# A convolution, attention and mixture-of-experts kernel: attention's matrix by halves of the channels, the norm's mean added to the residual by VectorE, the output's base made by ScalarE

## The chip, the cores and the metric

The kernel runs on one core of a Trainium2 chip. The metric is the device time in microseconds from the first to the last instruction. The core has a matrix engine (TensorE, PE in the profile, with its weight loads as PEld), a vector engine (VectorE, DVE), a scalar engine (ScalarE, ACT), a general one (GpSimd, POOL) and a queue that starts transfers (SyncE, SP). Each engine works through its own instructions in order, and they wait for one another through semaphores.

## The reference, cut to what matters

The input is 8 images of 56 x 56 pixels with 256 channels. Layer 0 is a convolution block: 32 parallel paths, each 256 to 4 channels, a 3 x 3 convolution, and back to 256, each step with a batch norm and a relu; the paths are summed and the input is added. Layer 1 reads its output as 3136 tokens for each image. The change lies in the middle of layer 1.

```python
x = relu(sum_of_paths(x) + x)                       # layer 0
t = x.reshape(8, 3136, 256)
n = ln(t)                                           # (t - mean) / sqrt(var + eps), over 256 channels
k = head_norm(n); v = head_norm(n)                  # 8 heads of 32 channels
kv = einsum('bhnd,bhne->bhde', k, v) / 3136         # one 32 x 32 matrix a head and image
t = t + einsum('bhnd,bhde->bhne', n, kv) + n        # attention, linear in n
u = ln(t)
t = t + u + sum_over_2_of_8_experts(gate * (gelu(u @ w1 + b1) @ w2 + b2))
```

Two facts carry the change. The attention's matrix, kv by heads with the identity added (A in the kernel), is block diagonal: a head of 32 channels reads only its own 32 channels, so output channels 0 to 127 need only input channels 0 to 127. And n = (t - mean) * rs1, so that A applied to n is rs1 * (t A) minus rs1 * mean * (the column sums of A): the mean can be taken into the matrix, or added afterwards as one row times one number for each token.

## The kernel before, in words

The work is cut into 56 chunks of 448 tokens (8 rows of pixels), seven for each image. A chunk lies in SBUF with tokens on the partitions, as 4 groups (k) of 112 tokens, or with channels on the partitions, as 2 halves (f) of 128.

The program is a loop over slots s = 0 to 64. In slot s the convolution's last product runs on chunk s (`conv3_steps`), its first product on chunk s + 2, its 3 x 3 product on chunk s + 1, the end of the convolution and the keys on chunk s - 1 (`end_steps`), and the attention on chunk a = s - 8 (`attn_steps`): an image's attention can only begin when all seven chunks of it have given their part of kv. `image_steps` makes A and its tables once an image, in the slot of its first chunk. `route_steps` chooses two experts for each token of the two chunks before, and scatters token rows to regions sorted by expert. `moe_steps` works through tiles of 256 such rows: transposes (te), two products (ph, py) with gelu between, and an indirect transfer by POOL that adds the result to the output rows. Slots 8 to 55 hold both convolution and attention; 56 to 64 hold attention and tiles alone; then only tiles are left.

Within a slot the order of PE, ACT and DVE is written out: `issue` (L1368) gives each part a stretch of the slot, spreads its steps over that stretch in proportion to their costs, and emits them sorted. The attention has 0.05 to 0.97 of a slot, or 0.35 to 0.97 in a slot that opens an image. POOL's and SP's orders are left to the framework. The three ordered engines then run strictly in that order, so a late step holds all that stands behind it on its engine.

The convolution's last product sets the beat. A `pair` (L577) is two products of 448 columns into two PSUM banks (c), a relu on ACT (L592) and a maximum and sum on DVE (L595) into r; `sum_paths` (L601) adds four r by a product (su), and when a half of the channels is done DVE adds bias and input (u, L615). Then `begin` (L643) is a relu of u on ACT, and `turn` (L655) transposes it on PE (tu). Seven PSUM banks serve all products except su.

The attention of one chunk, in `attn_steps`:
- `attend(k)`, four times: PE multiplies 112 tokens by the table tab of 256 + 16 columns (at, L870), once for each half f of the input channels, summed in PSUM. The table holds A with its column means taken off in all 256 columns, so the half away from the diagonal holds only the negative means. The last 16 columns are router logits. DVE multiplies by rs1 and adds the residual X (L874), ACT copies the logits (L878), and DVE takes mean and variance (L881, L882).
- After the fourth, POOL makes rs2 as a power of -0.5 (L885), and `means` makes nm = -mean * rs2 on DVE (L889).
- `normed(k)`: ACT writes the normed tokens to pay (L894), which is what routing scatters.
- `base`: POOL adds X and pay (L900) and SP stores the sum to the output (L902). The tiles later add their results to those rows.

`matrix` (L800) computes A's column means (cs) by a product with a constant matrix, A's transpose for the router, and fills the table with six DVE operations (L816, L818, L819).

Of the kernel before, what the change touches and what calls it, by code (L numbers as in the profile page):

```python
# [25 lines left out]
def kernel(  # L26
# [513 lines left out]

    below = const.tile([P, M, M], F32, name="below")
    nc.gpsimd.memset(below, 1.0)
# [89 lines left out]

    spilled, rs1s, kvs = {}, {}, {}
    G = KT * NH

    def end_steps(s):
# [58 lines left out]
        def variances():  # L695

            sd = v["sd"] = small([T, KT, NH + 1], "hsd")
            ss = small([T, KT, NH], "hss")
            nc.vector.tensor_reduce(
                ss, v["sq"].rearrange("q k (h c) -> q (k h) c", c=HC), AX.X, ALU.add  # L700
            )
            m = v["m"]
            mu = small([T, KT], "hmu")
            dm = small([T, KT, NH], "hdm")
            nc.vector.tensor_reduce(mu, m, AX.X, ALU.add)
            nc.vector.scalar_tensor_tensor(
                dm, mu[:, :, None].to_broadcast([T, KT, NH]), -1.0 / NH, m,
                op0=ALU.mult, op1=ALU.add,
            )
            nc.vector.tensor_mul(dm, dm, dm)  # L710
            nc.vector.scalar_tensor_tensor(
                dm, dm, float(HC), ss, op0=ALU.mult, op1=ALU.add
            )
            nc.vector.tensor_reduce(mu, dm, AX.X, ALU.add)
            nc.vector.tensor_scalar(
                sd[:, :, NH], mu, 1.0 / C, LN_EPS, ALU.mult, ALU.add
            )
            nc.vector.tensor_scalar_mul(sd[:, :, :NH], ss, 1.0 / (HC - 1))  # L718
            nc.gpsimd.tensor_tensor(  # L719
                sd, sd, half[:T, :].rearrange("q (k h) -> q k h", k=KT), ALU.pow  # L720
            )

        def inverse():
# [8 lines left out]
            rs1s[s] = keep.tile([T, KT], F32, tag="rs1", name=f"rs1_{s}")  # L732
            nc.vector.reciprocal(rs1s[s], sd[:, :, NH])

        def scale():
# [26 lines left out]

    tables_of = {}

    def image_steps(b):

        v = {}
# [32 lines left out]
        def matrix():  # L800
# [4 lines left out]
            for f in range(NF):  # L805
                nc.tensor.matmul(ps[:, f, :], mean_of, A[:, f, :], start=True, stop=True)
                nc.tensor.transpose(pt[:, f, :], A[:, f, :], ident)
            tab = v["tab"] = one.tile(
                [P, NF, C + 2 * E], F32, tag="tab", name=f"tab_{b}", bufs=2
            )  # L810
            nc.vector.tensor_copy(AT, pt)
            for f in range(NF):
                for g in range(NF):
                    dst = tab[:, f, g * P : (g + 1) * P]
                    if f == g:
                        nc.vector.tensor_sub(dst, A[:, g, :], ps[:, g, :])  # L816
                    else:
                        nc.vector.tensor_scalar_mul(dst, ps[:, g, :], -1.0)  # L818
                nc.vector.tensor_copy(tab[:, f, C + E :], rwc[:, f, :])  # L819

        def router():
# [13 lines left out]
            for f in range(NF):  # L835
                nc.vector.tensor_sub(tab[:, f, C : C + E], AR[:, f, :], pm[:, :E])
            tables_of[b] = tab

# [14 lines left out]
    def attn_steps(a):  # L853
        b, c = divmod(a, NCH)
        v = {}
        X, tT = Xs[a], fetched.pop(a)
        rs1 = rs1s.pop(a)
        lg = keep.tile([T, KT, 2 * E], F32, tag="lg", name=f"lg_{a}", bufs=4)
# [4 lines left out]
        nm = stat.tile([T, KT], F32, tag="nm", name=f"nm_{a}")  # L863
        late = []

        def attend(k):

            ps = ps_mm.tile([T, C + 2 * E], F32, tag="mm", name=f"at_{a}_{k}")
            for f in range(NF):
                nc.tensor.matmul(  # L870
                    ps, tT[:, f, k * T : (k + 1) * T], tables_of[b][:, f, :],
                    start=(f == 0), stop=(f == NF - 1),
                )
            nc.vector.scalar_tensor_tensor(  # L874
                X[:, k, :], ps[:, :C], rs1[:, k : k + 1], X[:, k, :],
                op0=ALU.mult, op1=ALU.add,
            )
            late.append(lambda: nc.scalar.copy(lg[:, k, :], ps[:, C:]))  # L878
            if k:
# [7 lines left out]
        def means():  # L887
            late.pop(0)()
            nc.vector.scalar_tensor_tensor(  # L889
                nm, mv[:, :, 0], -1.0, rs2, op0=ALU.mult, op1=ALU.mult  # L890
            )

        def normed(k):
# [3 lines left out]
            )  # L897

        def base():
            nc.gpsimd.tensor_add(X, X, pay[:, :, :C])  # L900
            del Xs[a]
# [7 lines left out]

        return (  # L910
            [(1.0, lambda k=k: attend(k)) for k in range(KT)]
            + [(0.6, means)]
            + [(0.4, lambda k=k: normed(k)) for k in range(KT)]
            + [(0.6, base)]
        )

# [10 lines left out]
    def route_steps(group):  # L927
# [10 lines left out]
        def logit():  # L938
            lg = v["lg"] = small([E], "rlg")
            for n, m in enumerate(group):  # L940
                _, raw, rs1, _ = pays[m]
                mine = lg[:, n * KT : (n + 1) * KT, :]
                nc.vector.tensor_tensor(
                    mine, raw[:, :, :E], rs1[:, :, None].to_broadcast([T, KT, E]), ALU.mult
                )
                nc.vector.tensor_add(mine, mine, raw[:, :, E:])

# [560 lines left out]
```

## Time and profile before

The three runs took 3394.81, 3409.42 and 3416.62 us; the median is 3409.42 us. The profiled execution has a span of 3400.0 us and a mean granted TensorE clock of 0.946.

| what | value |
|---|---|
| attention's products (at, L870) | 896 records, 265.7 us busy, mean 420 ns |
| their weight loads | 896 records, 148.8 us busy, mean 181 ns |
| residual on DVE (L874) | 224, 106.9 us, mean 477 ns |
| norm to pay on ACT (L894) | 224, 135.0 us, mean 604 ns |
| base on POOL (L900) | 56, 129.1 us, mean 2305 ns |
| power for rs2 on POOL (L885) | 56, 63.1 us, mean 1127 ns |
| r on DVE (L595) | 1792, 1127.3 us, mean 677 ns |
| r on ACT (L592) | 1792, 1031.9 us, mean 636 ns |

How to read the lines below. A row of the groups names line, engine, operation, output <- inputs, shapes and count; then the total busy time in us and the mean ns of one; then the idle time of that engine just before these instructions, with what ended most of it. A row of the stretches has start and end in us, the length, and for PE, PEld, DVE, ACT and POOL the busy us with the count of instructions, then granted clock, share of the transfer engines, and GB/s. A row of the waits says which instruction waited for which: total us, times, longest. A row of the timeline has start and length in us, engine, line, operation and tiles, how many alike were merged, and in brackets the idle time before and what ended it. Matmuls overlap, and their ends are modelled.

### The profile page before, as it was taken

The numbers are of one execution on the slowest core, as the hardware profiler recorded it, in microseconds if no ns is written. First come the engines' busy times: TensorE is split into PE (matmuls) and PEld (weight loads), VectorE is DVE, ScalarE is ACT, GpSimd is POOL, SyncE is SP. The second block draws the span as 40 slices with busy tenths as digits, with TensorE's granted clock in tenths as the row PEclk, the third lists the DMA queues.
The fourth block names the chain that finished last, engine by engine and source line by source line (L and its number), as shares of the span: only waits on it lengthen the run. The fifth ranks groups of instructions, "written<-read, shape, count | busy, mean of one in ns | idle before, by whom it ended". The sixth has DMA issues, their size and how long they took to land. (4 is left out here: it accounts for less than half of the span.)

```text
span 3400.0 us, 55203 instructions
## 1 busy us (share of the span) xinstructions
PE 3012.4 (89%) x16669; PEld 1697.1 (50%) x16669; DVE 2200.1 (65%) x5806; ACT 1894.1 (56%) x3799; POOL 1926.1 (57%) x1385
## 2 busy tenths in 40 slices
PE   5888888878999999999998999999999988788698
PEld 2333433333444554545455555455454545676587
DVE  4566777777777767776776777776777775333200
ACT  1555555546565665656665666566656655343345
POOL 2123234453456575656656566656656666777677
PEclk7999888889999999999998999999999999898899
DMA  5522244434556675666666676566666756788797
GB/s 119 136 83 79 77 113 122 123 101 143 147 150 158 163 186 160 173 159 175 167 167 173 155 199 182 153 174 180 168 168 158 189 149 176 174 224 220 178 224 177
DMA packets 341577, 537.72 MB, mean 158 GB/s; under 512 B 60048, under 2 KB 251680, under 8 KB 341280
## 3 DMA queue, kind: packets, MB, share of 16 engines
q1 hardware_dynamic: 257952, 430.73, 43.6%
q0 software_dynamic: 81984, 103.45, 16.8%
q8 instruction: 134, 2.20, 0.3%
q14 instruction: 163, 1.34, 0.1%
q10 hardware_dynamic: 1344, 0.02, 0.0%
HBM read 248.01 MB, written 192.55 MB: 130 GB/s over the span
## 5 line engine op out<-in xcount | busy, mean ns | idle before, releaser
L595 DVE SCALAR_TENSOR_TENSOR r<-c,nb,r 128x448 f32<-128x448 f32 x1792 | 1127.3, 677 | 563.0 <-ACT r L592 538.5
L592 ACT ACTIVATE r<-c,b3t 128x448 f32<-128x448 f32 x1792 | 1031.9, 636 | 394.8 <-PE c L587 378.1
L1325 POOL DMA_INDIRECT out_dram<-y,index x420 | 662.5, 1577 | 355.8 <-ACT y L1311 243.7
L587 PE MATMUL c<-hl,W3hl 64*128 64x448 f32 x3584 | 712.1, 431 | 71.8 <-ACT r L592 43.0
L608 PE MATMUL su<-r,gather 128*32 128x448 f32 x3584 | 582.0, 574 | 67.5 <-DVE r L595 67.1
L1031 POOL DMA_INDIRECT regions<-pay,rrowi x448 | 432.7, 966 | 322.2 <-PE c L587 211.4
L587 PEld LDWEIGHTS c<-hl,W3hl 64*128 64x128 f32 x3584 | 344.5, 190 | 507.7 <-issue 202.0
L1287 PE MATMUL ph<-eT,w 128*128 128x256 f32 x1680 | 462.4, 406 | 57.2 <-DMA w<-Wd 23.9
L1307 PE MATMUL py<-w,hT 128*128 128x256 f32 x1680 | 433.5, 383 | 0.0
L1311 ACT ACTIVATE y<-py,g 128x256 f32<-128x256 f32 x420 | 196.5, 474 | 398.0 <-PE py L1307 348.6
L1287 PEld LDWEIGHTS ph<-eT,w 128*128 128x128 f32 x1680 | 304.1, 197 | 196.9 <-issue 88.8
L719 POOL TENSOR_TENSOR hsd<-hsd,half 112x36 f32<-112x36 f32 x56 | 351.8, 6283 | 78.0 <-DVE hsd L718 77.6
L1291 ACT ACTIVATE hT<-ph,w 128x256 f32<-128x256 f32 x420 | 197.8, 476 | 300.2 <-PE ph L1287 180.9
L1307 PEld LDWEIGHTS py<-w,hT 128*128 128x128 f32 x1680 | 292.5, 192 | 28.2
L681 POOL TENSOR_TENSOR norm<-t,hmean 112x512 f32<-112x512 f32 x112 | 120.2, 1132 | 320.4 <-PE c L587 180.7
L870 PE MATMUL at<-tab,tT 128*112 128x272 f32 x896 | 265.7, 420 | 11.6 <-ACT y L1311 7.0
L608 PEld LDWEIGHTS su<-r,gather 128*32 128x32 f32 x3584 | 105.3, 110 | 275.9 <-DVE r L595 158.9
L262 PE MATMUL c<-R,W2t 96*32 96x448 f32 x1344 | 186.9, 573 | 13.2 <-DMA R<-h 11.8
L870 PEld LDWEIGHTS at<-tab,tT 128*112 128x112 f32 x896 | 148.8, 181 | 91.7 <-issue 16.3
L1303 PE MATMUL py<-b2hl,own 128*128 128x256 f32 x420 | 177.8, 423 | 18.5 <-ACT hT L1291 8.0
L894 ACT ACTIVATE pay<-X,nm,rs 112x256 f32<-112x256 f32 x224 | 135.0, 604 | 91.9 <-DVE nm L889 91.9
L976 POOL TENSOR_TENSOR rq<-ebase,rq 112x8 f32<-112x8 f32 (+1 forms) x32 | 52.9, 1654 | 197.7 <-DVE rq L975 197.7
(245 smaller groups left out, 3225.1 us busy)
## 6 DMA issues: line engine op xcount, KB each, us to landing
w<-Wd SPq DMA_DIRECT2D x210, 513.0 KB
rows<-regions SPq DMA_DIRECT2D x210, 259.0 KB
xi<-in_x_dram SPq DMA_DIRECT2D x56, 448.0 KB
hl<-hi SPq DMA_DIRECT2D x448, 56.0 KB
hl<-lo SPq DMA_DIRECT2D x448, 56.0 KB
tTs<-u SPq DMA_DIRECT2D x56, 448.0 KB
ts<-t SPq DMA_DIRECT2D x56, 448.0 KB
tT<-tTs SPq DMA_DIRECT2D x56, 448.0 KB
```

Source lines behind the costliest of these rows:

```text
L587: product = nc.tensor.matmul(tiles[g][:, :CH], W3hl[rows, ab, cg, :], hl[rows, ab, :], start=True, stop=True)
L592: nc.scalar.activation(r, tiles[0][:, :CH], AF.Relu, bias=b3t[:, cg, 2 * ab : 2 * ab + 1])
L595: nc.vector.scalar_tensor_tensor(r, tiles[1][:, :CH], nb3[:, cg, 2 * ab + 1 : 2 * ab + 2], r, op0=ALU.max, op1=ALU.add,)
L608: nc.tensor.matmul(ps[32 * c4 : 32 * c4 + 32, :CH], gather, unit.pop((s, 4 * u + c4)), start=(ab == 0), stop=(ab == NQ - 1),)
L719: nc.gpsimd.tensor_tensor(sd, sd, half[:T, :].rearrange("q (k h) -> q k h", k=KT), ALU.pow)
L870: nc.tensor.matmul(ps, tT[:, f, k * T : (k + 1) * T], tables_of[b][:, f, :], start=(f == 0), stop=(f == NF - 1),)
L1031: ins = nc.gpsimd.indirect_dma_start(out=regions[n], out_offset=bass.IndirectOffsetOnAxis(ap=v["row_i"][:, (m - group[0]) * KT + k, n : n ...
L1287: nc.tensor.matmul(ps, w[:, f * C + hf * P : f * C + (hf + 1) * P], eT[:, f, :], start=(f == 0), stop=(f == NF - 1),)
L1291: nc.scalar.activation(hT[:, hf, :], ps, AF.Gelu, bias=w[:, 2 * NF * C + hf : 2 * NF * C + hf + 1])
L1307: nc.tensor.matmul(ps, hT[:, f, h * P : (h + 1) * P], w[:, (NF + f) * C : (NF + f + 1) * C], start=False, stop=(f == NF - 1),)
L1311: nc.scalar.activation(y[:, h, :], ps, AF.Identity, scale=g[:, h : h + 1])
L1325: ins = nc.gpsimd.indirect_dma_start(out=out_rows, out_offset=at, in_=y[:, h, :], in_offset=None, compute_op=ALU.add, **partial,).ins
```

## The change: what it does and what it is for

Attention's matrix by halves. The table now holds, for each half f, only the 128 columns of its own diagonal block of A and the 16 logit columns, 144 in all. The two products of an attend no longer add up in PSUM: each writes its own 144 columns. The aim is fewer columns streamed by PE. The logits come in two halves, which `logit` adds on DVE.

The mean by VectorE. As A is stored without its means taken off, the means are added to the residual instead: `center` does X = cm * shift + X once for each k, where cm is the row of A's column means, the same on all partitions, and shift is -(sum of the token's channels) * rs1, made in `variances` and `inverse`. `matrix` then only copies.

The base by ScalarE. `raised(k)` computes X * (rs2 + 1) + nm, which is X plus its norm, on ScalarE in place of the addition on GpSimd; `up` is rs2 + 1. The steps' costs, by which `issue` places them, change with it: the four attends now fill a smaller part of the attention's stretch.

One constant of the planning (below) becomes bfloat16, which makes room in SBUF.

```diff
-    below = const.tile([P, M, M], F32, name="below")
+    below = const.tile([P, M, M], BF16, name="below")
...
+            v["sum"] = small([T, KT], "hsum")
+            nc.vector.tensor_scalar_mul(v["sum"], mu, -float(HC))
...
+            shifts[s] = keep.tile([T, KT], F32, tag="shift", name=f"shift_{s}")
+            nc.vector.tensor_mul(shifts[s], v["sum"], rs1s[s])
...
             nc.vector.tensor_copy(AT, pt)
-            for f in range(NF):
-                for g in range(NF):
-                    dst = tab[:, f, g * P : (g + 1) * P]
-                    if f == g:
-                        nc.vector.tensor_sub(dst, A[:, g, :], ps[:, g, :])
-                    else:
-                        nc.vector.tensor_scalar_mul(dst, ps[:, g, :], -1.0)
-                nc.vector.tensor_copy(tab[:, f, C + E :], rwc[:, f, :])
+            nc.vector.tensor_copy(cm, ps)
+            nc.vector.tensor_copy(tab[:, :, :P], A)
+            nc.vector.tensor_copy(tab[:, :, P + E :], rwc)
...
+        def center():
+
+            cm = tables_of[b][1].rearrange("q f c -> q (f c)")
+            for k in range(KT):
+                nc.vector.scalar_tensor_tensor(
+                    X[:, k, :], cm[:T], shift[:, k : k + 1], X[:, k, :],
+                    op0=ALU.mult, op1=ALU.add,
+                )
+
         def attend(k):
 
-            ps = ps_mm.tile([T, C + 2 * E], F32, tag="mm", name=f"at_{a}_{k}")
+            ps = ps_mm.tile([T, NF, NT], F32, tag="mm", name=f"at_{a}_{k}")
             for f in range(NF):
                 nc.tensor.matmul(
-                    ps, tT[:, f, k * T : (k + 1) * T], tables_of[b][:, f, :],
-                    start=(f == 0), stop=(f == NF - 1),
-                )
+                    ps[:, f, :], tT[:, f, k * T : (k + 1) * T], tables_of[b][0][:, f, :],
+                    start=True, stop=True,
+                )
+            mine = X[:, k, :].rearrange("q (f c) -> q f c", f=NF)
             nc.vector.scalar_tensor_tensor(
-                X[:, k, :], ps[:, :C], rs1[:, k : k + 1], X[:, k, :],
-                op0=ALU.mult, op1=ALU.add,
-            )
-            late.append(lambda: nc.scalar.copy(lg[:, k, :], ps[:, C:]))
+                mine, ps[:, :, :P], rs1[:, k : k + 1], mine, op0=ALU.mult, op1=ALU.add
+            )
+            late.append(lambda: nc.scalar.copy(lg[:, k], ps[:, :, P:]))
...
+            nc.vector.tensor_scalar_add(up, rs2, 1.0)
...
+        def raised(k):
+
+            nc.scalar.activation(
+                X[:, k, :], X[:, k, :], AF.Identity,
+                bias=nm[:, k : k + 1], scale=up[:, k : k + 1],
+            )
+
         def base():
-            nc.gpsimd.tensor_add(X, X, pay[:, :, :C])
...
         return (
-            [(1.0, lambda k=k: attend(k)) for k in range(KT)]
+            [(0.1, center)]
+            + [(1.0, lambda k=k: attend(k)) for k in range(KT)]
             + [(0.6, means)]
             + [(0.4, lambda k=k: normed(k)) for k in range(KT)]
-            + [(0.6, base)]
+            + [(0.4, lambda k=k: raised(k)) for k in range(KT)]
+            + [(0.1, base)]
         )
...
+                nc.vector.tensor_add(raw[:, :, 0], raw[:, :, 0], raw[:, :, 1])
```

More of the change, by code (lines that the diff above doesn't have):

```diff
@@ L630, in conv3_steps @@
         return steps
-    spilled, rs1s, kvs = {}, {}, {}
+    spilled, rs1s, shifts, kvs = {}, {}, {}, {}
     G = KT * NH
@@ L763 @@
     tables_of = {}
+    NT = P + 2 * E
     def image_steps(b):
@@ L807, in matrix @@
                 nc.tensor.transpose(pt[:, f, :], A[:, f, :], ident)
-            tab = v["tab"] = one.tile(
-                [P, NF, C + 2 * E], F32, tag="tab", name=f"tab_{b}", bufs=2
-            )
+            tab = v["tab"] = one.tile([P, NF, NT], F32, tag="tab", name=f"tab_{b}", bufs=2)
+            cm = v["cm"] = one.tile([P, NF, P], F32, tag="cm", name=f"cm_{b}", bufs=2)
             nc.vector.tensor_copy(AT, pt)
-            for f in range(NF):
-                for g in range(NF):
-                    dst = tab[:, f, g * P : (g + 1) * P]
-                    if f == g:
-                        nc.vector.tensor_sub(dst, A[:, g, :], ps[:, g, :])
-                    else:
-                        nc.vector.tensor_scalar_mul(dst, ps[:, g, :], -1.0)
-                nc.vector.tensor_copy(tab[:, f, C + E :], rwc[:, f, :])
+            nc.vector.tensor_copy(cm, ps)
+            nc.vector.tensor_copy(tab[:, :, :P], A)
+            nc.vector.tensor_copy(tab[:, :, P + E :], rwc)
         def router():
@@ L835, in router @@
             for f in range(NF):
-                nc.vector.tensor_sub(tab[:, f, C : C + E], AR[:, f, :], pm[:, :E])
-            tables_of[b] = tab
+                nc.vector.tensor_sub(tab[:, f, P : P + E], AR[:, f, :], pm[:, :E])
+            tables_of[b] = (tab, v["cm"])
         return [(1.0, keys), (1.5, matrix), (1.0, router)]
@@ L856, in attn_steps @@
         X, tT = Xs[a], fetched.pop(a)
-        rs1 = rs1s.pop(a)
-        lg = keep.tile([T, KT, 2 * E], F32, tag="lg", name=f"lg_{a}", bufs=4)
+        rs1, shift = rs1s.pop(a), shifts.pop(a)
+        lg = keep.tile([T, KT, NF, 2 * E], F32, tag="lg", name=f"lg_{a}", bufs=4)
         pay = payp.tile([T, KT, ROW], F32, tag="pay", name=f"pay_{a}")
@@ L863, in attn_steps @@
         nm = stat.tile([T, KT], F32, tag="nm", name=f"nm_{a}")
+        up = stat.tile([T, KT], F32, tag="up", name=f"up_{a}")
         late = []
+        def center():
[5 more added lines that the diff above has]
+                )
         def attend(k):
-            ps = ps_mm.tile([T, C + 2 * E], F32, tag="mm", name=f"at_{a}_{k}")
+            ps = ps_mm.tile([T, NF, NT], F32, tag="mm", name=f"at_{a}_{k}")
             for f in range(NF):
                 nc.tensor.matmul(
-                    ps, tT[:, f, k * T : (k + 1) * T], tables_of[b][:, f, :],
-                    start=(f == 0), stop=(f == NF - 1),
+                    ps[:, f, :], tT[:, f, k * T : (k + 1) * T], tables_of[b][0][:, f, :],
+                    start=True, stop=True,
                 )
+            mine = X[:, k, :].rearrange("q (f c) -> q f c", f=NF)
             nc.vector.scalar_tensor_tensor(
-                X[:, k, :], ps[:, :C], rs1[:, k : k + 1], X[:, k, :],
-                op0=ALU.mult, op1=ALU.add,
+                mine, ps[:, :, :P], rs1[:, k : k + 1], mine, op0=ALU.mult, op1=ALU.add
             )
-            late.append(lambda: nc.scalar.copy(lg[:, k, :], ps[:, C:]))
+            late.append(lambda: nc.scalar.copy(lg[:, k], ps[:, :, P:]))
             if k:
@@ L942, in logit @@
                 mine = lg[:, n * KT : (n + 1) * KT, :]
+                nc.vector.tensor_add(raw[:, :, 0], raw[:, :, 0], raw[:, :, 1])
                 nc.vector.tensor_tensor(
-                    mine, raw[:, :, :E], rs1[:, :, None].to_broadcast([T, KT, E]), ALU.mult
+                    mine, raw[:, :, 0, :E], rs1[:, :, None].to_broadcast([T, KT, E]), ALU.mult
                 )
-                nc.vector.tensor_add(mine, mine, raw[:, :, E:])
+                nc.vector.tensor_add(mine, mine, raw[:, :, 0, E:])
         dsc = desc[:T, None, :].to_broadcast([T, K, E])
```

## The prediction

> **What bounds the kernel now.** I read the page's shares first, then the busy time by stretches, then who PE waits for, then single slots of the timeline, and only then the rows of the lines that change.
>
> ```profile
> PE 3012.4 (89%) x16669; PEld 1697.1 (50%) x16669; DVE 2200.1 (65%) x5806; ACT 1894.1 (56%) x3799; POOL 1926.1 (57%) x1385
> ```
>
> The busiest engine is PE, but the mean hides stages. The busy time by stretches, with the columns PE, PEld, DVE, ACT, POOL, granted clock, DMA share and GB/s:
>
> ```profile
> 400.00:2800.00 2400.00, 2208.21 (x12551) 1156.58 (x12550) 1776.23 (x4529) 1435.95 (x2868) 1389.14 (x943) 0.96 0.60 158
> 3000.00:3200.00 200.00, 147.40 (x728) 124.78 (x727) 60.19 (x291) 78.04 (x178) 148.63 (x115) 0.86 0.77 200
> ```
>
> From 400 to 2800 us, the slots in which convolution and attention run together, PE is busy 92% and DVE 74%. From 2800 on, DVE is light, POOL and the DMA are busy three quarters of the time, and PE 74 to 89%. So PE work taken away counts in the first stretch, unless DVE is what a slot waits for. What PE waits for there (total us, times, longest):
>
> ```profile
> PE su L608 <- DVE r L595: 52.8, 32, 3.2
> PE c L587 <- ACT r L592: 27.1, 46, 2.6
> ```
>
> When PE stands, it mostly stands for DVE. One slot in two, about, shows why. In slots that route two chunks, DVE is nearly full for long stretches, here the first 10 us and then 1657 to 1667 us:
>
> ```profile
> 1642.50:1647.50 5.00, 5.00 (x32) 2.98 (x32) 4.68 (x16) 3.86 (x9) 1.24 (x1) 1.00 1.08 322
> 1647.50:1652.50 5.00, 5.00 (x27) 2.72 (x26) 4.76 (x15) 3.42 (x6) 0.00 (x0) 1.00 0.81 254
> 1657.50:1662.50 5.00, 4.78 (x28) 2.51 (x28) 4.82 (x12) 2.73 (x7) 2.35 (x3) 1.00 0.82 183
> 1662.50:1667.50 5.00, 4.48 (x20) 1.76 (x19) 4.86 (x17) 2.81 (x7) 2.46 (x4) 1.00 0.50 139
> ```
>
> The rows of what the change touches:
>
> ```profile
> L870 PE MATMUL at<-tab,tT 128*112 128x272 f32 x896 | 265.7, 420 | 11.6 <-ACT y L1311 7.0 <-ACT r L592 4.2
> L747 PE MATMUL kv<-norm 112*128 112x129 f32 x896 | 131.2, 306 | 21.2 <-DVE r L595 18.0 <-POOL norm L737 1.1 <-ACT r L592 0.3
> L894 ACT ACTIVATE pay<-X,nm,rs 112x256 f32<-112x256 f32 x224 | 135.0, 604 | 91.9 <-DVE nm L889 91.9
> L900 POOL TENSOR_TENSOR X<-X,pay 112x1024 f32<-112x1024 f32 x56 | 129.1, 2305 | 34.6 <-ACT pay L894 34.2
> L874 DVE SCALAR_TENSOR_TENSOR X<-at,rs,X 112x256 f32<-112x256 f32 x224 | 106.9, 477 | 69.6 <-PE at L870 69.3
> ```
>
> The attention's 448 matmuls show as 896 records: each float32 matmul runs as two. The kv row has the same count at 129 columns instead of 272, a near twin of the new width of 144.
>
> [...] the four records of one attend take 1.17 us with 0.39 us for one, so (1.17 - 0.39)/3 = 0.26 us apart[...]; sixteen of kv take 2.05 us, 0.116 us apart[...]. [...] small copies into pay (L1019) take 171 ns in the median and up to 3.0 us.
>
> **The change part by part.**
>
> *Halves on PE.* The two records of one product fall from 272 to 144 columns each. [...] by the slope between the two rows' spacings ((0.26 - 0.116)/143 = 1.0 ns a column) 129 ns and 115 us. I take 96, which is 1.71 us for each of 56 chunks. Of the chunks, 48 run beside the convolution and 8 in the tail.
>
> *Centre on VectorE.* Four new scalar_tensor_tensor of 112x256 per chunk, by the neighbour L874 0.48 us each: 1.9 us[...]. Five small operations come with it (the head sum, the shift, the raised scale, one addition of the two logit halves, each near 0.19 us or less): 0.7 us. Together 2.6 us on DVE for each chunk, 147 us in all. Where this lands decides the case. In the changed order the four stand right behind the slot's first two r and, in routing slots, six small logit operations, and in front of the u of L615. Behind u queue ScalarE's relu of it (L643), PE's turn of u (L655), and everything after on PE, which runs in order. Both kinds of slot, DVE rows first:
>
> ```profile
> 1700.39 0.68 DVE L615 SCALAR_TENSOR_TENSOR u<-su,sumb,xT 128x448 f32<-128x448 f32 x1
> 1702.70 1.28 DVE L595 SCALAR_TENSOR_TENSOR r<-c,nb,r 128x448 f32<-128x448 f32 x2 [1.64 <-ACT r L592]
> ...
> 1747.91 0.68 DVE L615 SCALAR_TENSOR_TENSOR u<-su,sumb,xT 128x448 f32<-128x448 f32 x1
> ```
>
> ```profile
> 1749.19 0.96 ACT L643 ACTIVATE u<-u 128x896 f32<-128x896 f32 x1
> ```
>
> ```profile
> 1750.73 0.65 PE L655 MATMUL tu<-ident,u 128*112 128x128 f32 x4 [0.75 <-ACT r L592]
> ```
>
> In the plain slot (1700 us) DVE stands idle 1.64 us right after u: the four additions cost nothing, hidden by that idle time. In the routing slot (1747 us) u ends at 1748.59 and ScalarE takes it 0.6 us later, PE's turn starts 0.58 us after ScalarE's end and has waited already. Put 1.9 us and two logit additions of 0.19 us ahead: u ends 2.3 us later, ScalarE 1.7 us later, PE's turn about 1.2 us later than now, and PE came there 0.43 us sooner, so it stands 1.6 us longer. That is the saving of 1.71 us, given back. In the slots that open an image the centre comes later, but into a stretch where DVE is also full; its 1.9 us are set against some 0.5 us that the shorter table saves (six operations, in the rows of L816, L818 and L819 two each of 277, 284 and 163 ns, 1.4 us an image, for two wide copies like L811's 0.41 us and one narrow). I count no gain there.
>
> *Base on ScalarE.* Four activations like pay's, 0.60 us each, 2.4 us a chunk, 135 us in all, on an engine busy 60% in the main stretch. They stand one by one between r, y and hT at the slot's end, where DVE has little to do; each can delay an r by 0.6 us, and I count nothing, with up to 0.5 us a slot in the range. POOL loses its addition of 2.3 us, 129 us in all, which in the main stretch nobody but the store waits for.
>
> *Tail.* Eight chunks save 1.71 us of PE, of which half counts with PE not the only limit: 7 us. There VectorE waits 82 us for the power of rs on POOL (L885), because that stands behind scatters and the old addition. Without the addition, and with the power some four scatters earlier in POOL's order in the routing slots, I count 6 us.
>
> *The rest*, the mask in bfloat16 and the wider logits, lies in small operations and costs nothing that shows.
>
> *Sum.* 21 plain slots at 1.71 us: 36. 20 routing and 7 opening slots: 0. Tail 7 + 6 = 13. 3409 - 49 = 3360 us.
>
> **The rivals.** *The whole gain comes* (chance 0.20): 96 us of PE, and 8 x 2.2 us of POOL in the tail, 3409 - 114 = 3295. For it: 92% PE. Against it: the routing slot above. *DVE and ScalarE take it all* (0.25): the plain slots give 36 us, but 0.5 us a slot of ScalarE's new work (24 us) comes back, and 3409 - 12 - 0 = about 3397. For it: PE waits for r from both engines. *Slower* (0.13): in routing and opening slots DVE is the bound and the full 2.6 us lands on the path: 27 x 2.6 = 70 us, less 36 us of the plain slots, 3443. For it: DVE at 4.7 to 4.9 of 5 us; against it: DVE runs idle again for 1.05 to 2.7 us within each such slot. My own case has 0.42.
>
> **How the numbers follow.** 3360 is the likeliest case. The lower end, 3295, is the full gain; the upper, 3430, lies between no change and the slower case, and leaves out most of that. Over 1% faster is below 3375: the full gain and most of my case, 0.54. Within 1% (to 3443): 0.31. Slower by more: 0.15.
>
> **What would show it.** The attention's records: 896 with 0.12 to 0.13 us between them, mean near 0.31 us. The centre's row: 224 of about 0.48 us. In plain slots DVE's idle time after u gone, and the slot about 1.7 us shorter; in routing slots PE waiting longer in front of the turn of u, and the slot as long as before. The wait of VectorE for the power in the tail below 82 us. I am wrong if routing slots shorten as well (then PE absorbed the late u), if plain slots don't, if the centre's additions take much more than 0.48 us beside POOL's work, or if the granted clock (0.96) moves by some per cent.

## The result, and the profile after

The changed kernel takes 3523.06 us in the median of four runs (3521.86 to 3525.01); the kernel before, run beside it, takes 3407.84. The ratio is 1.034, interval 1.031 to 1.038: 115 us slower, where 49 us faster was forecast.

First the shares of the page:

```profile
PE 3064.6 (87%) x16669; PEld 1729.8 (49%) x16669; DVE 2308.7 (66%) x6230; ACT 1996.1 (57%) x4023; POOL 1802.3 (51%) x1329
```

PE is busy 52 us longer than before, although its new products are shorter. The busy time by stretches, for the main stretch:

```profile
400.00:2800.00 2400.00, 2136.01 (x11851) 1122.26 (x11849) 1774.81 (x4632) 1443.14 (x2882) 1196.80 (x837) 0.94 0.56 149
```

In this stretch PE is busy 72 us less than before in the same one and finishes 700 records fewer, at a granted clock of 0.94 where it was 0.96. The groups of what changed:

```profile
L881 PE MATMUL at<-tab,tT 128*112 128x144 f32 x896 | 166.9, 310 | 0.3
...
L872 DVE SCALAR_TENSOR_TENSOR X<-cm,shift,X 112x256 f32<-112x256 f32 x224 | 99.6, 506 | 0.0
...
L913 ACT ACTIVATE X<-X,nm,up 112x256 f32<-112x256 f32 x224 | 133.2, 608 | 0.0
```

Each of these is close to the forecast: the products fell by 265.7 - 166.9 = 98.8 us, the additions take 0.51 us on average, ScalarE's part 133 us. What changed beside them is in the waits of the same stretch:

```profile
PE c L587 <- ACT r L592: 72.1, 59, 9.0
ACT pay L906 <- DVE nm L900: 59.1, 7, 10.0
PE su L608 <- DVE r L595: 53.0, 39, 4.0
...
PE tu L655 <- ACT r L592: 35.0, 15, 2.4
```

The last of these waits was this before:

```profile
PE tu L655 <- ACT r L592: 10.4, 14, 0.8
```

PE stands longer for ScalarE's r (the first row was 27.1 us before), and ScalarE for nm (28.4 us before). To see where, I cut the trace at the first of the 64 products c of each slot and summed the slots by kind: those that open an image, plain ones, those that route two chunks, and routing ones before an opening. The last column is the time within slots 8 to 55 that the trace's clock record gives at half clock; slot 55 ends with its last product c. Each row is one profiled execution; in slots 0 to 7, which have no attention, the kernels differ by -4 to +7 us. Lengths of before in us, then differences to it:

| kernel | 0-7 | 8-14 | opening (6) | plain (18) | routing (12) | routing, next opens (5) | tail | half clock |
|---|---|---|---|---|---|---|---|---|
| before | 327.0 | 323.0 | 392.5 | 842.7 | 645.4 | 257.7 | 553.9 | 191 |
| after | +5.0 | +25.3 | +39.9 | +20.7 | +28.9 | +16.7 | -16.4 | 297 |
| costs only (e1) | +1.9 | +12.0 | +21.4 | +6.6 | +22.3 | +5.8 | +3.2 | 256 |
| old places (e2) | +5.8 | +16.9 | +18.8 | +2.1 | +36.1 | +23.1 | -15.8 | 348 |
| halves only (e5) | -3.8 | -3.4 | +12.9 | +2.8 | +0.6 | +5.8 | +1.0 | 287 |
| base only (e6) | -3.6 | -2.1 | +11.7 | +11.2 | -9.0 | +1.0 | -14.9 | 198 |
| centre only (e7) | -0.8 | +3.6 | +8.7 | +4.8 | +20.4 | +7.8 | +5.3 | 205 |
| centre in the gap (i1) | +6.8 | +2.1 | +16.5 | +23.6 | +2.5 | +9.9 | -17.3 | 236 |
| warm openings (i3) | +3.3 | -7.4 | -9.5 | +1.9 | -2.7 | +0.7 | -8.1 | 109 |

**A routing slot of after** (28), on VectorE, ScalarE and PE, and the stretches over the same time:

```profile
1438.92 1.67 DVE L872 SCALAR_TENSOR_TENSOR X<-cm,shift,X 112x256 f32<-112x256 f32 x4
1440.50 0.68 DVE L615 SCALAR_TENSOR_TENSOR u<-su,sumb,xT 128x448 f32<-128x448 f32 x1
...
1441.21 0.95 ACT L643 ACTIVATE u<-u 128x896 f32<-128x896 f32 x1 [1.41 <-DVE u L615]
1442.07 1.14 ACT L592 ACTIVATE r<-c,b3t 128x448 f32<-128x448 f32 x2
...
1439.38 0.94 PE L587 MATMUL c<-hl,W3hl 64*128 64x448 f32 x4
1442.74 0.65 PE L655 MATMUL tu<-ident,u 128*112 128x128 f32 x4 [2.42 <-ACT r L592]
1443.32 1.96 PE L608 MATMUL su<-r,gather 128*32 128x448 f32 x8
1445.21 2.56 PE L225 MATMUL c<-xT,W1s 128*128 128x448 f32 x4
```

```profile
1441.00:1443.00 2.00, 0.26 (x2) 0.27 (x3) 1.86 (x8) 1.79 (x3) 0.00 (x0) 1.00 1.05 312
1443.00:1445.00 2.00, 2.00 (x12) 0.47 (x10) 1.86 (x7) 0.79 (x2) 0.00 (x0) 0.60 0.80 293
1445.00:1447.00 2.00, 2.00 (x4) 0.99 (x4) 1.90 (x6) 0.00 (x0) 0.00 (x0) 0.54 0.01 4
1447.00:1449.00 2.00, 2.00 (x14) 1.27 (x12) 0.78 (x7) 1.20 (x3) 1.40 (x1) 1.00 0.00 0
```

The four additions stand ahead of u; ScalarE waits 1.41 us for u, its r stands behind, and PE waits 2.42 us where the kernel before waited 0.75. The new thing follows: of the next four microseconds some 3.4 are at half clock (0.60 and 0.54 in the two stretches), su takes 1.96 us and c 2.56. In the routing slot of before that the prediction shows, these two followed the turn of u like this:

```profile
1751.31 0.96 PE L608 MATMUL su<-r,gather 128*32 128x448 f32 x8
1752.20 1.77 PE L225 MATMUL c<-xT,W1s 128*128 128x448 f32 x4
```

So the wait is paid twice, once standing and once in slow products.

**An opening slot of after** (36, from 48.1 us after its start), on POOL, VectorE, ScalarE and PE:

```profile
1926.91 6.17 POOL L722 TENSOR_TENSOR hsd<-hsd,half 112x36 f32<-112x36 f32 x1
...
1935.60 1.64 POOL L896 TENSOR_TENSOR rs<-rs,mhalf 112x4 f32<-112x4 f32 x1
...
1937.27 0.16 DVE L900 SCALAR_TENSOR_TENSOR nm<-mv,rs 112x4 f32<-112x4 f32 x1 [3.35 <-POOL rs L896]
...
1937.47 0.60 ACT L906 ACTIVATE pay<-X,nm,rs 112x256 f32<-112x256 f32 x1 [5.52 <-DVE nm L900]
...
1938.64 1.26 PE L587 MATMUL c<-hl,W3hl 64*128 64x448 f32 x2 [5.61 <-ACT pay L906]
1939.84 2.07 PE L1308 MATMUL ph<-eT,w 128*128 128x256 f32 x4
```

Power of hsd, a scatter and an indirect addition, power of rs, nm, pay, r, product: one chain, and PE stands 5.61 us. Here too the products behind the wait are slow, ph takes 2.07 us at a granted clock of 0.50 (1938 to 1942 us).

### The profile page after: what moved, and what is told of

It reads as the page before. It is cut to its first block, busy times and chain, and to the rows that moved or that the text cites. A ratio compares the mean times of both kernels' runs of the same rounds, so it can differ in the third digit from the quotient of the medians.

```text
span 3520.2 us, 55737 instructions
## 1 busy us (share of the span) xinstructions
PE 3064.6 (87%) x16669; PEld 1729.8 (49%) x16669; DVE 2308.7 (66%) x6230; ACT 1996.1 (57%) x4023; POOL 1802.3 (51%) x1329
## 5 line engine op out<-in xcount | busy, mean ns | idle before, releaser
L587 PE MATMUL c<-hl,W3hl 64*128 64x448 f32 x3584 | 775.2, 435 | 119.5 <-ACT r L592 90.2
L608 PE MATMUL su<-r,gather 128*32 128x448 f32 x3584 | 629.6, 590 | 97.8 <-DVE r L595 72.3
L587 PEld LDWEIGHTS c<-hl,W3hl 64*128 64x128 f32 x3584 | 370.7, 191 | 553.6 <-ACT r L592 240.3
L1308 PE MATMUL ph<-eT,w 128*128 128x256 f32 x1680 | 471.8, 413 | 25.5 <-ACT hT L1312 7.6
L1328 PE MATMUL py<-w,hT 128*128 128x256 f32 x1680 | 440.9, 388 | 0.0
L681 POOL TENSOR_TENSOR norm<-t,hmean 112x512 f32<-112x512 f32 x112 | 121.6, 1164 | 329.8 <-PE c L587 132.5
L608 PEld LDWEIGHTS su<-r,gather 128*32 128x32 f32 x3584 | 115.7, 111 | 327.4 <-DVE r L595 169.3
L262 PE MATMUL c<-R,W2t 96*32 96x448 f32 x1344 | 193.1, 556 | 13.5 <-DMA R<-h 11.2
L881 PEld LDWEIGHTS at<-tab,tT 128*112 128x112 f32 x896 | 124.2, 182 | 95.2 <-issue 45.2
L881 PE MATMUL at<-tab,tT 128*112 128x144 f32 x896 | 166.9, 310 | 0.3
```

The costliest lines, as they stand in the source:

```text
L587: product = nc.tensor.matmul(tiles[g][:, :CH], W3hl[rows, ab, cg, :], hl[rows, ab, :], start=True, stop=True)
L608: nc.tensor.matmul(ps[32 * c4 : 32 * c4 + 32, :CH], gather, unit.pop((s, 4 * u + c4)), start=(ab == 0), stop=(ab == NQ - 1),)
L881: nc.tensor.matmul(ps[:, f, :], tT[:, f, k * T : (k + 1) * T], tables_of[b][0][:, f, :], start=True, stop=True,)
L1308: nc.tensor.matmul(ps, w[:, f * C + hf * P : f * C + (hf + 1) * P], eT[:, f, :], start=(f == 0), stop=(f == NF - 1),)
L1328: nc.tensor.matmul(ps, hT[:, f, h * P : (h + 1) * P], w[:, (NF + f) * C : (NF + f + 1) * C], start=False, stop=(f == NF - 1),)
```

## The experiments

Each ratio is to the kernel before, run beside it, with its 95% interval. That kernel's median lay between 3398.9 and 3407.8 us from one set of runs to the next, so small differences between sets are better read from the ratios.

**Where the steps stand (e1 to e4).** The change also altered the list of step costs, and so where every step of the attention stands. e1 gives the kernel before the new list, with empty steps in place of the new ones:

```
-            [(1.0, lambda k=k: attend(k)) for k in range(KT)]
+            [(0.1, lambda: None)]
+            + [(1.0, lambda k=k: attend(k)) for k in range(KT)]
...
-            + [(0.6, base)]
+            + [(1.6, lambda: None)]
+            + [(0.1, base)]
```

> The kernel before with nothing changed but the attention's list of step costs: the list of the changed kernel, with empty steps where centre and raised stand (0.1 and 1.6). No instruction is added or taken away; attends, means and normed move earlier in the slot. Theory 'placement' (the steps moved to where PE, ACT and POOL cannot follow): 60 to 100 us slower than before, 3470 to 3510, most of it in the slots that open an image (ScalarE holding its first pay until the power of rs2 is there). Rival 'work' (VectorE's and ScalarE's added work is what costs): within 1% of before, 3375 to 3440.

3475.92 us, ratio 1.0224 (1.0207 to 1.0241). The list alone costs 77 us: opening slots 3.6 us each, where pay's first activation again stands ahead of r and waits for the power, routing slots 1.9.

e2 is the changed kernel with a list that puts the steps where they stood:

```
-            [(0.1, center)]
+            [(0.0, center)]
...
-            + [(0.4, lambda k=k: raised(k)) for k in range(KT)]
-            + [(0.1, base)]
+            + [(0.15, lambda k=k: raised(k)) for k in range(KT)]
+            + [(0.0, base)]
```

> The changed kernel with the attends, means and normed back at their places of before (centre costs 0.0, raised 0.15 each, base 0.0, the sum 6.8 as before). All of the new work stays. Theory 'placement': 60 to 100 us faster than the changed kernel, 3420 to 3465; the slots that open an image lose their extra 7 us, the routing slots keep the late u. Rival 'work': no different from the changed kernel, 3500 to 3535.

3487.82 us, 1.0259 (1.0242 to 1.0276). It lies between the two expectations: only 35 us come back, or 26 when each kernel is set against the kernel before beside it. Placement and the rest overlap; a cost of 89 us remains at the old places.

e3 keeps the new list and puts each addition directly ahead of its own residual; e4 does both:

```
+            center(k)
             mine = X[:, k, :].rearrange("q (f c) -> q f c", f=NF)
```

> The changed kernel with its step costs, but each of the four centre operations stands directly before the residual's operation of its own attend, so none stands before u. Theory 'late u' (the four in front of u hold ScalarE's relu of u and PE's turn of it): the routing slots lose the 2.9 us that they gain up to the turn of u, 20 x 2.9 = 58 us, so about 3465; plain and opening slots stay. Rival 'work' (VectorE is full in those slots wherever the operations stand): 3505 to 3535.

> The changed kernel with both edits: old places for the attention's steps, and each centre operation directly before its own residual operation. All of the change's work stays. Theory 'placement and late u': the saving of PE shows, 3350 to 3400, faster than before. Rival 'work': 3480 to 3530, the work is the same.

3528.63 us (1.038, 1.0361 to 1.0398) and 3514.95 us (1.0347, 1.0328 to 1.0366). Neither is as the theory of the late u had it. Most of the lateness is gone (the first u of a routing slot starts 5.7 us into it in e2, 4.1 in e3 and 3.6 before), but plain slots are 46 and 54 us longer over 18: the additions now stand ahead of other r's, and VectorE's hinv comes 2 us later in these slots. Moving the work along a full order only moved what it holds up.

**One part at a time (e5 to e8).** e5 is the halves alone (without the mean's term), e6 ScalarE's base alone, e7 the additions alone (with a row of zeros, and without the small operations that make the shift), e8 the change without ScalarE's base; all at the old places. For e7:

```
+                nc.vector.scalar_tensor_tensor(
+                    X[:, k, :], zero, rs1[:, k : k + 1], X[:, k, :],
+                    op0=ALU.mult, op1=ALU.add,
+                )
```

> The kernel before with the products by halves alone: two products of 144 columns in place of two of 272, the old step costs, the base on POOL, no addition of the mean (so the norm's mean is left out of the residual, and the output differs). If PE bounds the slots, as the prediction has it, 48 x 1.71 = 82 us go from the slots and some 7 from the tail: 3310 to 3340. If PE waits for r, u and the banks whatever it does itself, and its saving is spent waiting: 3375 to 3400, with the attention's records near 0.31 us all the same.

> The kernel before with its base made by ScalarE alone (four activations of 112x256 a chunk, POOL's addition gone), at costs that leave the other steps where they stood. If VectorE's added work is what costs, and ScalarE has room: 3385 to 3405, the tail a few us shorter. If ScalarE's four 0.6 us delay r and hT (rival), 1 to 2 us a slot: 3440 to 3490.

> The kernel before with VectorE's four additions alone: 4 scalar_tensor_tensor of 112x256 a chunk that add a row of zeros, ahead of the attends, at a cost of 0. If the late u is what costs, 20 routing slots by 3.3 us and opening slots by 3: 3460 to 3500, with plain slots unchanged. If PE's later work makes up for it (rival): 3400 to 3420.

> The changed kernel at the old places with its base on POOL as before: halves and centre without ScalarE's part. If VectorE's part costs and ScalarE's doesn't: 3470 to 3490, as with ScalarE's base at the same places (3488). If ScalarE's base is what costs there (rival): 3380 to 3410. If parts add up, the difference from before is that of halves alone plus that of the centre alone.

Measured: e5 3422.30 (1.0052, 1.0031 to 1.0074), e6 3397.16 (0.9978, 0.9966 to 0.9990), e7 3455.00 (1.0155, 1.0115 to 1.0195), e8 3509.64 (1.0310, 1.0274 to 1.0347). The halves bring nothing, they cost 16 us, more than either expectation had. ScalarE has room for the base, near enough: the tail is 15 us shorter by that alone, and all other slots together 9 us longer. The additions cost 48 us. And 16 + 48 is 64, while the two together (e8) cost 103: halves and additions make each other worse by some 40 us, which no theory so far explains. e8 also lies above its expectation of 3470 to 3490, as the base on POOL leaves the tail as long as before.

Why the halves bring nothing in a plain slot, the PE rows of before and of e5 at the same place show:

```profile
1867.94 0.68 PE L587 MATMUL c<-hl,W3hl 64*128 64x448 f32 x4
1868.55 1.17 PE L870 MATMUL at<-tab,tT 128*112 128x272 f32 x4
1869.65 0.73 PE L587 MATMUL c<-hl,W3hl 64*128 64x448 f32 x4
1870.31 1.13 PE L1287 MATMUL ph<-eT,w 128*128 128x256 f32 x4
```

```profile
1874.11 0.68 PE L587 MATMUL c<-hl,W3hl 64*128 64x448 f32 x4
1874.72 0.74 PE L864 MATMUL at<-tab,tT 128*112 128x144 f32 x4
1875.39 1.16 PE L587 MATMUL c<-hl,W3hl 64*128 64x448 f32 x4
1876.48 1.13 PE L1289 MATMUL ph<-eT,w 128*128 128x256 f32 x4
```

The attend is 0.43 us shorter, and the next four products are 0.43 us longer: from c to ph it is 2.37 us in both. The products stop in mid-group (the second four c take 1.16 us, not 0.73) and the trace counts that as busy. The program has seven rotating PSUM tiles (`ps_mm`, L73), so by the order of the code the fourth product of this group takes the bank of the second product of the group before, which r on VectorE reads last. In e5 that read ends 1.92 us after the first c above, at 1876.03, and the fourth product's record starts at 1876.08. (The third starts at 1875.89, also late, which this does not explain.) In before the read also ends 1.92 us after the first c, but PE, later there, has nothing to wait for. Over e5 the attends' records lose 97.0 us of busy time, but the c records gain 34.5, su 13.4, ph 9.7, py 9.4, and PE's sum falls by 19.3 us only. Part of that gain is the slower clock (287 us of half clock against 191); the plain slots of the next group of runs set it aside.

**POOL's own order (f0, f5, f2).** POOL's order is the framework's. In opening slots, counted from POOL's last subtraction of the mean (L681), it put hsd's power behind 5 or 6 scatters in before and in e6, behind 6 or 7 in e5, and behind 7 or 8 in after, e2 and e8; and e5's opening slots lose 2.2 us each, just behind that power. The next three tie it, by an order without a wait behind the last power written out:

```
                 tc.add_manual_dep(ins, pace[0].name, SYNC, reason="spread over the slot")
+                behind(ins)
```

> The kernel before with POOL's order tied: each scatter and each indirect addition that is written out after a power (hsd or rs) stays behind that power on POOL. The framework arranges POOL's order itself, and did it differently in each kernel so far: in slots that open an image the power of hsd stood behind 5 scatters before, behind 7 or 8 in most changed kernels. A control: 3380 to 3420, opening slots within 2 us of before.

> Halves alone (the mean's term left out of the residual) with POOL's order tied in the same way. If the halves' loss of 16 us came from POOL's other order, this is at or below the tied kernel before: 3370 to 3400, its opening slots no longer than there. If it comes from the lower granted clock or from PE's own order (rival): 10 to 20 us above it.

> The three parts at the old places with POOL's order tied. If the late u of the routing slots is what remains (20 of them by some 3 us): 3440 to 3470, opening slots as before. If POOL's order is without effect (rival): 3480 to 3495, as it was untied.

f0 3419.31 (1.0042, 1.0024 to 1.0060), f5 3422.72 (1.0053, 1.0036 to 1.0070), f2 3488.95 (1.0252, 1.0224 to 1.0281). The tie itself costs the kernel before 16 us, so the tied kernels are read against f0. Halves then cost 3 us, inside the noise, and their opening slots are 4 us below f0's in sum, where e5's were 13 us above before: POOL's order made that part of e5's loss, and the halves are worth nothing rather than less. The plain slots of f0 and f5 have the same half clock, 14 us over the 17 from slot 15 to 54. There the attends' records lose 29 us, the c records gain 13, su and the 3 x 3 product 5, PE's idle time grows by 7, and the slots are 3 us shorter. So the saved time goes into stops and waits there also where the clock plays no part. f2's opening slots are back to 3 us over before in sum (19 in e2), but its plain slots give that back (25 us over before, 2 in e2; in f0 the tie costs 9 there). So POOL's order does not explain f2's 70 us over f0.

**The late u (i1).** The additions for the next chunk stand one slot earlier, ahead of hinv, where VectorE waits for hsd's power anyway (46 waits, 74.9 us in before); for an image's first chunk they stay:

```
-            (1.8, variances), (0.8, inverse),
+            (1.8, variances), (0.0, lambda: ahead(s + 1 - NCH)), (0.8, inverse),
```

> The same with the four additions of the mean for the next chunk, except an image's first, placed on VectorE right in front of hinv, where it waits for POOL's power of hsd (6.2 us) anyway, one slot before the attends. If VectorE's work costs only where something stands behind it: 3370 to 3410, routing slots without a late u. If VectorE's work costs wherever it stands (rival, as when it stood before each residual): 3440 to 3480.

3444.00 us, 1.0117 (1.0086 to 1.0148), between the two expectations: 45 us below f2. The routing slots gain more than that (+66 us over before in f2, +12 here), while opening slots lose some (+3 and +17). So for a routing slot the place of the same four additions is worth over 3 us. They are not free where they stand now: the kernel is still 40 us above before, 24 of it in plain slots.

**The clock (g1, g2, g3, i2, i3, h1).** The time from a slot's first product c to its thirteenth, in six routing slots, with the half clock within it in brackets:

| kernel | 21 | 24 | 28 | 31 | 35 | 38 |
|---|---|---|---|---|---|---|
| before | 10.6 | 10.6 | 10.6 | 10.6 | 10.6 | 10.6 |
| centre only (e7) | 11.8 | 11.8 | 11.8 | 12.1 | 11.8 | 11.8 |
| old places (e2) | 14.1 (3.4) | 14.8 (6.8) | 14.0 (3.4) | 12.3 | 13.7 (3.4) | 15.1 (6.8) |
| centre in the gap (i1) | 11.2 | 10.7 | 10.7 | 10.7 | 10.7 | 10.7 |
| g3 | 12.8 | 12.3 | 12.3 | 12.3 | 12.3 | 12.3 |

At full clock the late u costs 12.3 - 10.6 = 1.7 us, with half clock 3.1 to 4.5. g1 adds constant products ahead of the turn of u, g2 issues each half twice, g3 repeats the last product c ahead of the wait eight times into its own place:

```
+            if step == 5 and g == 1 and s > NCH and (s - NCH - 1) % NCH in (2, 4, 6):
+                for _ in range(8):
+                    product = nc.tensor.matmul(
+                        tiles[g][:, :CH], W3hl[rows, ab, cg, :], hl[rows, ab, :],
+                        start=True, stop=True,
+                    )
```

> The three parts at the old places, with 7 constant products of 128 columns (1.6 us of PE) added in front of the first turn of u in the 20 routing slots, where PE waits 2.4 us for the late u; their result is overwritten. If half the late u's cost is PE's half clock after that wait: some 1.5 us a routing slot less, 3450 to 3470, no half clock 7 to 9 us into routing slots. If the late u itself is all (rival): 3485 to 3500.

> The three parts at the old places with every half's product issued twice into the same place, so that the attends take PE 1.5 us each again and not 0.74. If the saved PE time only lengthens waits and lowers the clock: 3440 to 3480, below the 3488 of the same kernel with each product once. If PE's time counts (rival): 3510 to 3560.

> The three parts at the old places; in the routing slots the last product of the convolution in front of the first turn of u is issued 8 more times into its own place, so that PE works during the first part of its 2.4 us wait (the constant products of the run before had to wait for the same bank as the turn itself, and so came after the wait). If the half clock after this wait costs: no half clock 7 to 10 us into routing slots, 10 to 30 us below 3488. If the late r and u are all (rival): 3485 to 3510.

g1: 3516.34 (1.0337, 1.0309 to 1.0365), 28 us worse than e2. Its ScalarE and PE rows say why:

```profile
1608.25 1.14 ACT L592 ACTIVATE r<-c,b3t 128x448 f32<-128x448 f32 x2
...
1608.92 2.29 PE L654 MATMUL tu<-ident 128*112 128x128 f32 x14 [2.42 <-ACT r L592]
1611.00 1.06 PE L658 MATMUL tu<-ident,u 128*112 128x128 f32 x4
```

The constant products need nothing of u, yet they wait the same 2.42 us, until the first half of ScalarE's r: PE waits there for r, as the trace names it, by the order of the code by way of the bank, and r stands behind u on ScalarE. The filling came after the wait, so g1 says nothing on the clock. g2: 3504.05 (1.0290, 1.0263 to 1.0317), which meets neither expectation: against e2 the 17 routing slots of the table have 65 us at half clock and not 119, but are only 3 us shorter in sum, and plain slots are 16 us longer. Its attends take 1.23 us each in the median, more than the 1.17 of before. g3 does what g1 was to do; its PE rows in slot 28 with the stretches, after those of e2 in the same slot:

```profile
1428.25 0.65 PE L655 MATMUL tu<-ident,u 128*112 128x128 f32 x4 [2.42 <-ACT r L592]
1428.83 1.56 PE L608 MATMUL su<-r,gather 128*32 128x448 f32 x8
1430.32 3.06 PE L225 MATMUL c<-xT,W1s 128*128 128x448 f32 x4
```

```profile
1430.00:1434.00 4.00, 4.00 (x13) 2.20 (x12) 3.11 (x15) 0.59 (x1) 0.89 (x1) 0.63 0.23 87
```

```profile
1425.51 1.78 PE L592 MATMUL c<-hl,W3hl 64*128 64x448 f32 x8
1428.08 0.65 PE L661 MATMUL tu<-ident,u 128*112 128x128 f32 x4 [0.80 <-ACT r L598]
1428.66 1.20 PE L614 MATMUL su<-r,gather 128*32 128x448 f32 x8
1429.79 1.77 PE L225 MATMUL c<-xT,W1s 128*128 128x448 f32 x4
```

```profile
1430.00:1434.00 4.00, 4.00 (x20) 2.55 (x19) 3.08 (x15) 2.40 (x5) 1.05 (x1) 1.00 0.10 29
```

The turn starts as late as in e2, but the clock stays at 1.00 and c takes 1.77 us instead of 3.06. No half clock falls into these stretches in any of the six slots above. As a whole g3 is at 3488.43 (1.0257, 1.0222 to 1.0292), no faster. In slots 26, 33, 47 and 54 the wait lies inside that group of products, the repeats come after it, and the thirteenth product comes at 16.7 to 18.4 us instead of 13.6 to 16.7. Over all 20 routing slots the first thirteen products still take 10 us less than in e2, and other parts of the program lose that again, 7 us of it in opening slots; why, no run isolates. That the late u brings the half clock, and the half clock the slow products, is shown; the version is no gain.

i2 leaves ScalarE's base only to the last seven chunks; i3 adds constant products into three waits of PE in opening slots; h1 is i3 with the halves (and without the mean's term):

```
+                warm(ps[:, f, :], 7)
                 nc.tensor.matmul(ps[:, f, :], ones_f, rows, start=True, stop=True)
...
+            warm(pm[:, :P], 5)
```

> The kernel before with its base made by ScalarE only for the last 7 chunks, after the convolution has ended, and by POOL as before for the others. If the tail's gain of 15 us in the changed kernel is POOL's relief alone: 3385 to 3395. If it needs the halves as well (rival): 3398 to 3408.

> The same with constant products in three waits of PE in each slot that opens an image: 7 in front of each of the two sums over the keys, 5 in front of the router's mean. If the half clock after those waits (3.4 to 10 us in each such slot) delays the slot: 15 to 30 us below the kernel with ScalarE's base in the tail alone, 3355 to 3380. If not (rival): equal to it or up to 10 us slower.

> Halves alone (the mean's term left out of the residual) with ScalarE's base in the tail and the constant products in the waits of the opening slots, to be read against the same without halves (3377). POOL's order in opening slots is that of halves alone, which cost some 13 us there. If the lower clock ate the halves' 82 us: 3320 to 3360. If banks and the chain of r through ScalarE and VectorE set the slots: 3370 to 3395.

i2 3393.40 (0.9970, 0.9958 to 0.9981). i3 3377.40 (0.9917, 0.9895 to 0.9939): it beats both kernels, 16 us by products that compute nothing. The start of slot 36 in before and in i3, PE's rows and the stretches:

```profile
1798.77 0.76 PE L782 MATMUL sv<-Arow,ones_f 128*128 128x128 f32 x2 [1.93 <-DVE Arow L781]
1801.63 0.80 PE L782 MATMUL sv<-Arow,ones_f 128*128 128x128 f32 x2 [2.10 <-DVE A L786]
1802.22 1.91 PE L1287 MATMUL ph<-eT,w 128*128 128x256 f32 x4
```

```profile
1801.00:1805.00 4.00, 3.37 (x14) 1.81 (x14) 2.77 (x10) 0.47 (x1) 0.55 (x1) 0.50 0.97 262
```

```profile
1783.40 1.74 PE L768 MATMUL sv<-ident 128*128 128x128 f32 x14
1785.40 0.49 PE L789 MATMUL sv<-Arow,ones_f 128*128 128x128 f32 x2 [0.26 <-issue]
...
1788.46 1.03 PE L1307 MATMUL ph<-eT,w 128*128 128x256 f32 x4
```

```profile
1787.00:1791.00 4.00, 4.00 (x32) 2.74 (x33) 3.72 (x13) 0.52 (x2) 0.49 (x1) 1.00 1.06 326
```

With the wait filled, ph takes 1.03 us and not 1.91. POOL's order in opening slots is the same in i2, i3 and before. h1 is at 3383.47 (0.9932, 0.9908 to 0.9955), 6 us above i3, inside the noise: with the openings filled the halves still give nothing. Its half clock is 191 us in slots 8 to 55, and i3's 109. That the saved PE time turned into waits, and the waits into half clock, fits this but is not shown: h1 also has the other POOL order of e5.

## Why the prediction was wrong, step by step

*Halves on PE, 96 us.* The size was right (98.8 us of records, mean 310 ns as forecast); that it was 96 and not the 115 of the slope was my estimate, which no trace of before showed. My reading of the spacing was not quite: the median from one record of an attend to the next is 229 ns before and 123 ns after, 0.83 ns a column, and the 0.26 us came from the first record of each group, which takes longer (483 ns against 392, and 320 ns to the next record; 377, 286 and 213 after). A weight load of 112 columns shows as 177 ns in the median, before and after. The step that failed is "So PE work taken away counts in the first stretch" with its 36 us for plain slots. Alone the halves gain nothing (e5, f5 against f0, h1 against i3); the plain slots gain 3 us of the 36 in f5 against f0, and lose 3 in e5. The 92% on which I built contained PE's stops within groups of products: of the 541 unbroken groups of four c at full clock from 400 to 2800 us in before, whose median is 0.68 us, 63 took over 0.90 us (after: 123 of 434). The proviso "unless DVE is what a slot waits for" was the case, as far as the stop above shows it: a bank, and r on VectorE behind it.

*Centre in plain slots, nothing.* Right: +0.3 us a slot in e7. (I counted five small operations beside it; there are four in each chunk.)

*Centre in routing slots, "it stands 1.6 us longer. That is the saving of 1.71 us, given back".* The longer wait was right: 2.42 - 0.75 = 1.67 us. Two things were wrong. There was no saving to give back, and the wait brings half clock with it, 3.4 or 6.8 us long: the twelve slots lose 36 us in e2 and the five before an opening 23, so 3.5 us each. This explains the larger part of the 40 us that halves and centre cost together beyond their sum. In 14 of the 20 routing slots the turn waits as a whole: with the centre alone PE waits 1.73 to 1.80 us there and falls to half clock within the first thirteen products in 3 of the 14, with both 2.42 us and in 13 (e2). Of the 40 us some 25 lie in these first thirteen products (e8 against e5 and e7); some more lie in slots 0 to 7, where e7 makes no shift. I also took the turn's wait as one for u; the trace names r, and g1's products, which need nothing of u, wait the same 2.42 us. By the order of the code that is r's bank; r follows u, so the time is the same.

*Opening slots, "I count no gain there".* They lost 6.7 us each. I weighed only VectorE's work. What the runs show there is the new list, which puts pay ahead of r while nm still waits for POOL (e1: 3.6 us), POOL's other order, with hsd's power starting 46.7 us into the slot instead of 41.7 (with that order tied, in f2, opening slots lose 0.5 us each, in e2 3.1), and half clock in and after the wait of 5.6 us (0.62 from 1934 to 1938 us and 0.50 to 1942 in slot 36). Their shares of the 6.7 us overlap and were not separated further.

*The list of costs* I did not price at all, and alone it costs 77 us (e1). It was the largest single edit.

*Base on ScalarE, nothing beside the convolution.* Nearly right: 9 us over all its slots (e6).

*Tail, 13 us.* The sum came near (16.4), but by luck, for the split was wrong: the tail is 1.0 us longer with the halves alone (e5) and 14.9 us shorter with ScalarE's base alone (e6). It is POOL's relief alone. VectorE's wait for rs in the tail fell from 82.1 to 61.5 us as I said, but in e5, whose tail is no shorter, it fell to 62.9 as well, so it is no sign of the gain.

*The clock.* I named a move of it as what would make me wrong, and gave it no case. In the clock records of before and after the half-clock periods of slots 8 to 55 are 3.41 us long or two to four times that, and there is chance in what a wait brings: with the same wait of 2.41 to 2.42 us the thirteen products of after took 12.3 us in slots 21, 24 and 31, and 13.9 to 14.8 in 28, 35 and 38. Little idle time can be enough: in slot 36 of before the clock fell 1.6 us into the wait of 1.93 us. What goes with it can be counted, as far as the modelled ends of the products allow. All changes of the clock in these slots lie on one grid of 3.41 us in each of the two traces. Of the 93 stretches of this grid at full clock in slots 8 to 55 of the two in which PE was busy less than 0.6, 73 were followed by one at half clock; of the 1152 in which it was busy 0.8 or more, none. So a wait of 2.42 us that falls into one stretch leaves PE busy at most 0.29 of it, and one of 1.75 us 0.49; cut by the grid, a wait leaves more in each of the two. Shorter products and longer waits both lower that share, which fits the fall of the clock in e5 and after, though no run isolates it.

*What stays open.* Plain slots lose 1.1 us each in after and 1.3 in i1, which no run isolates; so do slots 0 to 7, 3 to 7 us in the kernels that compute the shift, where the others lie between -4 and +3. That the fourth product of a group waits for VectorE's read of just that bank follows from the code's order and the times, and was not tried with another number of banks. The rival *Slower* named routing and opening slots, which did lose most, but with neither the list nor the clock in its reasons, and it still gave the plain slots their 36 us.

## What to carry to other kernels

A busy matrix engine need not be a bound: compare a group of products with its own shortest length at the same clock, and if it is longer, the time between may belong to another engine, and work saved ahead of it can be lost in it. Price a wait of PE like the 2.42 us of these slots twice, once for itself and once for the slow products after it; filling it with useless products can pay (i3, 16 us), if they need no bank that the wait is for (g1). And an edit of the order is an edit: run the new order with empty steps before any of the work.

## What the runs showed of the hardware

Products that compute nothing made a kernel 16 us faster (i3 against i2), with half clock in slots 8 to 55 down from 188 to 109 us. Useless products behind a wait, in contrast, cost time: g1 is 28 us slower than e2, and 14 records of 128 columns, 1.74 us at full clock in i3, took 2.29 there, where the granted clock fell to 0.62 and 0.50. On POOL a power of 112x36 took 6.17 us and one of 112x4 1.64 us in the same opening slot (6.16 and 1.05 in the median of 56), and the chain to pay and PE's next product went through both. VectorE's additions took 0.48 us in the median, but four of 224 took 1.3 to 2.9 us.
